# Residual sums of layers 1 and 2: VectorE, or ScalarE and GpSimd

## The chip, the cores and the metric

The kernel runs on one core of a Trainium2 chip. The metric is the device time of one launch in microseconds (us). The kernel before took 6616.1 us, the median of three runs (6615.68 to 6616.88). Differences under 0.2% (13 us) are not told from no change.

The engines are called TensorE (PE in the profile, its weight loads PEld), VectorE (DVE), ScalarE (ACT), GpSimd (POOL) and SyncE (SP). SP here only issues DMAs.

## The reference

Four graph layers over 16 graphs of 1024 nodes with 128 features, each followed by a residual sum and a layer norm. Layers 1 and 2 are the ones concerned.

```python
# layer 1: maximum over the neighbours
def _L1_gnn_ref(x, adj, W, b):
    W1, W2 = (W[:d], W[d:])
    p = einsum('bnd,do->bno', x, W1 - W2)
    q = einsum('bnd,do->bno', x, W2)
    pre = p[:, :, None, :] + q[:, None, :, :] + b
    return max(relu(pre) * adj[..., None], axis=2)

# layer 2: sum over the neighbours, two dense layers
def _L2_gnn_ref(x, adjacency, node_mask, W1, b1, W2, b2, eps):
    x_agg = einsum('bnf,bnm->bmf', x, adjacency)
    h = (1.0 + eps) * x + x_agg
    y = maximum(h @ W1 + b1, 0.0) @ W2 + b2
    return where(node_mask[..., None], y, 0)

x = _layernorm(x + _L0_gnn_ref(...))   # attention over the neighbours
x = _layernorm(x + _L1_gnn_ref(...))
x = _layernorm(x + _L2_gnn_ref(...))
x = _layernorm(x + _L3_gnn_ref(...))   # three SAGE convolutions on a thinned adjacency
```

Layer 3 first thins the adjacency: node by node, in order, each node drops every so-many-th of its remaining neighbours, and a dropped edge vanishes for later nodes too. This thinning depends on the adjacency alone. The kernel calls it the dilation.

## The kernel before, in words

The kernel has a long first stage, in which layers 0, 1 and 2 and the dilation run together, and a second stage for layer 3. The change lies in the first stage.

**The slot loop.** The maximum over neighbours of layer 1 takes most of the work. Its columns are cut into 86 groups (NP) of 12 nodes for each graph, and one group is one slot: 16 x 86 = 1376 slots. In each half of a slot (512 nodes) TensorE selects rows of a table of subset maxima by matrix product (`look_up`, L779, tile pg, two PSUM buffers of two banks), and VectorE folds the result into a running maximum (`best`, L831, 128x1024). TensorE also counts which subset each node needs (L748, tile pm) and ScalarE turns the count into a selection (L749, tile hot, three buffers, made two slots ahead). ScalarE splits the table into a high and a low part (L763, L770).

**Fillers between the slots.** All other work is written as Python generators that are drawn on between the slots. While graph b is in the slot loop, `scores` and `attend` do layer 0 of graph b+1, `tables_of` builds its subset tables on VectorE (L467), and `rest` finishes layers 1 and 2 of graph b-1. A generator asks for an engine before each operation, with an estimated cost; `advance` lets it go on when the slot has room left for that engine (ROOM), when a delay in slots has passed since its last step (0.5 unless `delay` says otherwise, 0 with `same=True`), and, for a product in PSUM, when one of two shared banks is free. So the order of instructions on PE, ACT, DVE and POOL is written out by hand by this planner, from estimates, before the kernel runs; each engine then works through its own list in order. The order on SP is not written out.

**`rest`, the generator that is changed.** It relus the layer 1 maximum (L389), transposes it in two halves of four 128x128 blocks into a shared bank (L395), and adds X on VectorE (L398) into y. `norm` takes statistics on VectorE (L265, eight bn_stats), works out the factors on GpSimd in ten small operations (`norm_factors`, L219 to L228), and normalises on ScalarE (L270, eight activations, asked for 6.5 slots after the factors). For layer 2, X is split into three bf16 parts (L408 on ScalarE, L411 on GpSimd), multiplied by the adjacency (L419, L422), and put through two dense layers (L286, L440). The product py lies in a shared bank in two halves; VectorE multiplies it by the node mask nm (L443) and adds X (L445). `norm` follows again, and the result is stored.

**The dilation on GpSimd.** The nodes are walked in 32 rounds of 32 rows, each round about 43 slots, so two rounds go by in a graph. VectorE prepares a round's counts (L601, L603). GpSimd then walks 31 rows in a chain of small dependent operations (L616 to L626, ten operations for each row):

```python
gp.tensor_scalar(half, mine, half_mask[:, m], rest[:, n:n + 1], op0=ALU.mult, op1=ALU.add)
...
gp.tensor_sub(low[:, n + 1:], low[:, n + 1:], hit[:, n, n + 1:])
```

SP stores the result (L632) and loads it back in another layout (L635, tile hit_p), and VectorE goes on with its transpose (L639), which the planner places about nine slots after the last row. With the next counts (L603) the next round begins.

**The last graph.** When the slot loop ends, `rest` of graph 15 has nothing to run beside: it is drawn on 15 times, then the last of the dilation, then the remainder, and layer 3 begins with the edges of graph 0 (L891, L902, L906).

Of the kernel before, what the change touches and what calls it, by code (L numbers as in the profile page):

```python
# [34 lines left out]
AF = mybir.ActivationFunctionType  # L35
# [4 lines left out]
B, N, D, H2 = 16, 1024, 128, 256  # L40
P = 128
# [30 lines left out]
def tile_graph_layers(ctx: ExitStack, tc, a, out):  # L72
    nc = tc.nc
# [77 lines left out]
    def four(v):  # L151
        return v.unsqueeze(1).to_broadcast([3, 4, P])
# [7 lines left out]
    nm = consts.tile([P, T, B], F32, name="nm")  # L160
# [6 lines left out]
    for b in range(B):  # L167
        q, g = divmod(b, G)
# [19 lines left out]
    X = {}  # L188
# [25 lines left out]
    def norm_factors(st):  # L214

        mv = small.tile([P, 4, T], F32, name="ln_mv")
        mean, apart, var, rs = (mv[:, i, :] for i in range(4))
        gp = nc.gpsimd
        gp.tensor_add(mean, st[:, :, 1], st[:, :, 4])  # L219
        gp.tensor_sub(apart, st[:, :, 1], st[:, :, 4])  # L220
        gp.tensor_scalar(mean, mean, -0.5, 0.0, op0=ALU.mult, op1=ALU.add)
        gp.tensor_mul(apart, apart, apart)
        gp.tensor_add(var, st[:, :, 2], st[:, :, 5])
        gp.tensor_scalar(var, var, 1.0 / D, LN_EPS, op0=ALU.mult, op1=ALU.add)
        gp.tensor_scalar(apart, apart, 0.25, 0.0, op0=ALU.mult, op1=ALU.add)
        gp.tensor_add(var, var, apart)
        gp.tensor_tensor(rs, var, mhalf, op=ALU.pow)
        gp.tensor_mul(mean, mean, rs)  # L228
        return rs, mean
# [6 lines left out]
    def layers_012():  # L236
# [17 lines left out]
        def ask(engine, cost, take=False, give=False, same=False, delay=0.5, after=None, third=False, urgent=False):  # L254
            return engine, cost, take, give or urgent and None, 0 if same else delay, after, third

        def shared(name):
            return psum.tile([P, 512], F32, tag="shared", name=name, bufs=2)


        def norm(dst, src):
            st = small.tile([P, T, 6], F32, name="ln_st")
            for t in range(T):
                yield ask("V", 0.29, same=True)
                nc.vector.bn_stats(out=st[:, t, :], in_=src[:, t, :])  # L265
            yield ask("Pool", 0)
            rs, mean = norm_factors(st)
            for t in range(T):
                yield ask("A", 0.25, same=(t > 0), delay=6.5)
                nc.scalar.activation(dst[:, t, :], src[:, t, :], AF.Identity, bias=mean[:, t:t + 1],  # L270
                                     scale=rs[:, t:t + 1])

        def columns_of(dst, src, first=0.5):
            for h in range(2):
                yield ask("PE", 0.44, take=True, delay=0.5 if h else first)
                p = shared("ptr")
                for t in range(4):
                    nc.tensor.transpose(p[:, t * P:(t + 1) * P], src[:, 4 * h + t, :], ident)
                yield ask("A", 0.59, give=True, same=True)
                nc.scalar.copy(dst[:, halves[h]], p)  # L280

        def product_of(lhsT, rhs, dst, func, bias, delay=0.5):
            for h, s in enumerate(halves):
                yield ask("PE", 0.86, take=True, delay=0.5 if h else delay)
                p = shared("pp")
                nc.tensor.matmul(p, lhsT, rhs[:, s], start=True, stop=True)  # L286
                yield ask("A", 0.6, give=True, same=True)
                if bias is None:
                    nc.scalar.copy(dst[:, s], p)  # L289
                else:  # L290
                    nc.scalar.activation(dst[:, s], p, func, bias=bias)
# [94 lines left out]
        def rest(b):  # L386
            best = ps.pop(b)
            yield ask("A", 1.06, after=("rest", b - 1) if b else None)
            nc.scalar.activation(best, best, AF.Relu)  # L389
            y = w4.tile([P, T, D], F32, name="y1", tag="y")  # L390
            for h in range(2):
                yield ask("PE", 0.44, take=True)
                pt = shared("ph")
                for t in range(4):
                    nc.tensor.transpose(pt[:, t * P:(t + 1) * P],  # L395
                                        best[:, (4 * h + t) * P:(4 * h + t + 1) * P], ident)
                yield ask("V", 0.66, give=True)
                nc.vector.tensor_add(y[:, 4 * h:4 * h + 4, :], X[b][:, 4 * h:4 * h + 4, :],  # L398
                                     pt.rearrange("p (t d) -> p t d", d=D))
            happened["y1", b] = now  # L400
            yield from norm(X[b], y)
            xT = w4.tile([P, N], F32, name="xT2")
            yield from columns_of(xT, X[b])
            left = w4.tile([P, T, D], F32, name="left", tag="y")
            parts = w4.tile([P, 3, T, D], BF, name="parts")
            for k in range(3):
                yield ask("A", 1.05, delay=2.5 if k else 0.5)
                nc.scalar.copy(parts[:, k], left if k else X[b])  # L408
                if k < 2:
                    yield ask("Pool", 0)  # L410
                    nc.gpsimd.tensor_sub(left, left if k else X[b], parts[:, k])  # L411
            hT = w4.tile([P, N], F32, name="hT")
            for h, s in enumerate(halves):
                for c in range(T):
                    yield ask("PE", 0.65, take=(c == 0), same=(c > 0))
                    if c == 0:
                        pa = shared("pa")
                    for k in range(3):
                        nc.tensor.matmul(pa, parts[:, k, c, :], An[b][:, c, s], start=(c == 0 and k == 0),  # L419
                                         stop=(c == T - 1 and k == 2))  # L420
                yield ask("V", 0.66, give=True)
                nc.vector.scalar_tensor_tensor(hT[:, s], xT[:, s], eps1, pa, op0=ALU.mult, op1=ALU.add)  # L422
            del An[b]
            zT = []
            for k, tag in ((0, "xT2"), (1, "parts")):
                z = w4.tile([P, N], F32, name=f"z{k}", tag=tag)
                yield from product_of(W1[:, k * P:(k + 1) * P], hT, z, AF.Relu, b1[:, k:k + 1])
                zT.append(z)
            y = w4.tile([P, T, D], F32, name="y")
            for h in range(2):  # L430
                q = slice(4 * h, 4 * h + 4)
                for half in range(2):
                    yield ask("PE", 1.0, take=(half == 0), same=(half == 1))
                    if half == 0:
                        py = shared("py").rearrange("p (t d) -> p t d", d=D)
                        nc.tensor.matmul(py, ones_b[:3, :], four(b23), start=True, stop=False)
                    for t in range(2 * half, 2 * half + 2):
                        own = slice((4 * h + t) * P, (4 * h + t + 1) * P)
                        for k in range(2):
                            nc.tensor.matmul(py[:, t, :], zT[k][:, own], W2[:, k, :],  # L440
                                             start=False, stop=(t == 3 and k == 1))
                yield ask("V", 0.65, give=True)
                nc.vector.tensor_mul(y[:, q, :], py, nm[:, q, b].unsqueeze(2).to_broadcast([P, 4, D]))  # L443
                yield ask("V", 0.65)
                nc.vector.tensor_add(y[:, q, :], y[:, q, :], X[b][:, q, :])  # L445
            yield from norm(X[b], y)
            nc.sync.dma_start(out=x3[b], in_=X[b])
            happened["rest", b] = now
# [32 lines left out]
        def dilation():  # L481
# [100 lines left out]
            for k in range(K):  # L582
# [18 lines left out]
                nc.vector.tensor_copy(low, p[:B, 0:R])  # L601
                rest = dil.tile([B, R], F32, name="rest")
                nc.vector.scalar_tensor_tensor(rest, p[:B, R:2 * R], 0.5, half_mask[:, own], op0=ALU.add, op1=ALU.mult)  # L603
                given[own_bank] = now + 0.5
                work = [behind]
# [247 lines left out]
        with tc.manual_schedule(engines={mybir.EngineType.PE, mybir.EngineType.Activation, mybir.EngineType.DVE,  # L853
# [3 lines left out]
            finish(B)  # L857
        assert not streams, streams
        last = rest(B - 1)
        for _ in range(15):  # L860
            next(last)
# [21 lines left out]
    def rows_bank(name):  # L883
        return psum.tile([P, 4, D], F32, tag="subset", name=name, bufs=2)
# [246 lines left out]
    for b in range(B):  # L1131
# [3 lines left out]
        for h in range(2):  # L1135
            p = rows_bank("pback")
# [33 lines left out]
```

## Time and profile before

| what | value |
|---|---|
| median of three runs | 6616.1 us |
| profiled execution | 6613.2 us |
| its span | 6611.5 us |
| mean granted TensorE clock | 0.904 |
| stretch of the slot loop | about 137 to 5284 us |
| VectorE, busy share of the span | 80% |
| TensorE, busy share of the span | 86% |
| GpSimd, busy share of the span | 58% |
| ScalarE, busy share of the span | 56% |
| L831, the running maximum | 2720 of 1210 ns |

The shares are means over the whole span; the first stage and layer 3 load the engines quite differently. In the lines shown below, a group of instructions reads: line, engine, operation, what is written and read, shapes, count, then the busy time in us and the mean in ns, then the idle time just before and what ended it. A wait reads: who, waited for whom, us in total, times, longest. A timeline line reads: start in us, length in us, engine, line, operation, tiles, and in brackets the idle time before it. A stretch reads: from and to, its length, then busy us of PE, PEld, DVE, ACT and POOL with counts, the granted clock, the share of the DMA engines, and GB/s.

### The profile page before, as it was taken

How to read it: one execution, taken by the hardware profiler on the slowest of the kernel's cores; microseconds unless marked ns; L12 is line 12 of the kernel's file. 1: busy time of each engine (PE TensorE's matmuls, PEld its weight loads, DVE VectorE, ACT ScalarE, POOL GpSimd, SP SyncE). 2: the span in 40 equal slices, each digit the busy share in tenths (PEclk: the TensorE clock that was granted, in tenths of full speed). 3: DMA queues.
4: the chain of work that ended last, by engine and by line, in shares of the span. 5: the costliest groups of instructions: out<-in, count | busy, mean ns of one | idle time of the engine just before them, and what ended most of it. 6: DMA issues, size and time to landing. Idle time of an engine off the chain costs nothing. (4 is left out here: it accounts for less than half of the span.)

```text
span 6611.5 us, 85916 instructions
## 1 busy us (share of the span) xinstructions
PE 5697.7 (86%) x27306; PEld 2883.8 (44%) x27306; DVE 5317.7 (80%) x8130; ACT 3733.9 (56%) x6537; POOL 3844.7 (58%) x11285
## 2 busy tenths in 40 slices
PE   6989898989898989899888898888888768787986
PEld 3434344444444444444444444444443345555643
DVE  3989899999999999999999999999998834444453
ACT  4656566666666666666666656666655523333841
POOL 2675767676767776766666676767676511110126
PEclk8989898989898989898989899999987779888997
DMA  5121212121212121212112212121110156563635
GB/s 37 14 27 22 30 24 36 20 27 26 28 28 27 27 27 26 28 26 31 28 29 30 27 26 27 26 27 28 25 25 9 32 93 120 105 124 102 230 128 166
DMA packets 478381, 317.02 MB, mean 48 GB/s; under 512 B 301162, under 2 KB 429668, under 8 KB 473828
## 3 DMA queue, kind: packets, MB, share of 16 engines
q0 software_dynamic: 105648, 84.20, 14.6%
q1 hardware_dynamic: 367600, 226.13, 11.7%
q8 instruction: 214, 3.51, 0.2%
q10 hardware_dynamic: 4676, 1.19, 0.1%
q14 instruction: 243, 1.99, 0.1%
HBM read 412.71 MB, written 117.18 MB: 80 GB/s over the span
## 5 line engine op out<-in xcount | busy, mean ns | idle before, releaser
L831 DVE TENSOR_TENSOR best<-best,pg 128x1024 f32<-128x1024 f32 x2720 | 3234.4, 1210 | 309.0 <-PE pg L779 300.5
L749 ACT ACTIVATE hot<-pm,one_less 128x512 fp32r<-128x512 f32 x2752 | 1882.3, 688 | 1115.1 <-PE pm L748 1102.9
L779 PE MATMUL pg<-hot,high 64*128 64x512 f32 x5504 | 1479.1, 534 | 453.6 <-DVE best L831 417.8
L779 PE MATMUL pg<-hot,low 64*128 64x512 f32 x5504 | 1173.3, 423 | 0.0
L748 PE MATMUL pm<-AT,lit 120*128 120x512 fp8e4 x2752 | 1143.8, 416 | 9.3 <-ACT hot L749 6.2
L779 PEld LDWEIGHTS pg<-hot,high 64*128 64x128 f32 x5504 | 547.9, 196 | 1265.1 <-DVE best L831 792.4
L616 POOL TENSOR_SCALAR sc<-low_counts,half_mask,rest 16x1 f32<-16x1 f32 x992 | 435.7, 439 | 399.6 <-DVE rest L603 305.8
L779 PEld LDWEIGHTS pg<-hot,low 64*128 64x128 f32 x5504 | 573.4, 205 | 0.0
L748 PEld LDWEIGHTS <-lit 120*128 120x128 fp8e4 x2752 | 274.5, 100 | 624.8 <-issue 560.8
L621 POOL TENSOR_SCALAR sc<-sc 16x1 f32<-16x1 f32 x992 | 430.1, 434 | 105.0
L770 ACT CAST low<-pt 128x256 fp32r<-128x256 f32 x688 | 255.6, 371 | 396.3 <-PE pt L768 392.1
L980 POOL TENSOR_TENSOR length<-length,mhalf 128x8 f32<-128x8 f32 x48 | 78.9, 1644 | 571.7 <-DVE length L979 571.7
L618 POOL TENSOR_SCALAR sc<-sc 16x1 f32<-16x1 f32 x992 | 341.8, 345 | 107.7
L624 POOL TENSOR_SCALAR last_rank<-V,sc 16x31 f32<-16x31 bf16 (+30 forms) x992 | 387.1, 390 | 0.0
L623 POOL TENSOR_SCALAR hit<-V,sc 16x31 bf16<-16x31 bf16 (+30 forms) x992 | 372.5, 376 | 0.0
L768 PE MATMUL pt<-high,less 128*128 128x256 f32 x688 | 303.2, 441 | 66.3 <-ACT high L763 58.9
L467 DVE TENSOR_TENSOR sub<-sub,q 128x24 f32<-128x24 f32 (+11 forms) x768 | 306.6, 400 | 24.6 <-ACT q L289 10.5
L619 POOL TENSOR_SCALAR sc<-sc 16x1 f32<-16x1 f32 x992 | 270.1, 272 | 83.3
L937 ACT CAST m<-near 128x1024 fp32r<-128x1024 fp8e4 x256 | 253.3, 1044 | 112.7 <-DVE near L906 59.8
L760 PE MATMUL pt<-ident,sub 128*128 128x128 f32 x1376 | 293.9, 298 | 24.7 <-ACT hot L749 22.0
L377 PE MATMUL pav<-v,eT 128*128 128x128 f32 x2048 | 307.6, 296 | 2.1 <-ACT eT L370 2.1
L617 POOL TENSOR_SCALAR sc<-sc 16x1 f32<-16x1 f32 x992 | 256.6, 259 | 86.6
(258 smaller groups left out, 9495.7 us busy)
## 6 DMA issues: line engine op xcount, KB each, us to landing
removed<-gone SPq DMA_DIRECT2D x128, 256.0 KB
An<-in_adj_dram POOLq DMA_DIRECT2D x16, 1024.0 KB, 15.1
E<-in_adj_dram POOLq DMA_DIRECT2D x128, 128.0 KB, 6.8
gone_all<-removed POOLq DMA_DIRECT2D x64, 256.0 KB, 12.1
near<-in_adjT_dram POOLq DMA_DIRECT2D x16, 1024.0 KB, 17.3
h<-x SPq DMA_DIRECT2D x32, 512.0 KB
kept<-near SPq DMA_DIRECT2D x16, 1024.0 KB
share<-share SPq DMA_DIRECT2D x32, 512.0 KB
```

Of the source, the lines that this page charges most:

```text
L377: nc.tensor.matmul(pav, eT[:, c, :], values[b][:, c, :], start=(c == 0), stop=(c == T - 1))
L467: nc.vector.tensor_max(sub[:, :n_g, n:2 * n], sub[:, :n_g, 0:n], qg[:, 2 * g0:2 * g0 + n_g, k:k + 1].to_broadcast([P, n_g, n]))
L616: gp.tensor_scalar(half, mine, half_mask[:, m], rest[:, n:n + 1], op0=ALU.mult, op1=ALU.add)
L618: gp.tensor_scalar(sf, half, 5.5, sf, op0=ALU.is_gt, op1=ALU.mult)
L621: gp.tensor_scalar(to, at, sf, none, op0=ALU.subtract, op1=ALU.subtract)
L623: gp.tensor_scalar(hit[:, n, n + 1:], V[:, n, n + 1:], at, None, op0=ALU.is_equal)
L624: gp.tensor_scalar(last[:, n + 1:], V[:, n, n + 1:], to, None, op0=ALU.is_le)
L748: nc.tensor.matmul(pm, lit[:, r, :], AT[b * (T + 1) + c][:, halves[h]], start=True, stop=True)
L749: nc.scalar.activation(hots[s][:, halves[h]], pm, AF.Relu, bias=one_less)
L768: nc.tensor.matmul(pt, less, high, start=False, stop=True, skip_group_check=True)
L779: nc.tensor.matmul(pg[:, a], part[rows, at * P:(at + 1) * P], hots[s][rows, halves[h]], start=(k == 0), stop=(k == 1))
L831: nc.vector.tensor_max(own, own, pg)
```

## The change

In layer 1, ScalarE copies the transposed maximum from PSUM into y, and GpSimd adds X in place. In layer 2, ScalarE multiplies py by the node mask while it takes it from PSUM, one activation for each of the four 128-column blocks because the mask is a scale for each partition, and GpSimd adds X in place. Before each `norm`, a request for VectorE with a delay of four slots is put in. Nothing else is edited; the planner lays out the other work anew.

```diff
@@ rest, layer 1
-                yield ask("V", 0.66, give=True)
-                nc.vector.tensor_add(y[:, 4 * h:4 * h + 4, :], X[b][:, 4 * h:4 * h + 4, :],
-                                     pt.rearrange("p (t d) -> p t d", d=D))
+                yield ask("A", 0.6, give=True, same=True)
+                q = slice(4 * h, 4 * h + 4)
+                nc.scalar.copy(y[:, q, :], pt.rearrange("p (t d) -> p t d", d=D))
+                yield ask("Pool", 0)
+                nc.gpsimd.tensor_add(y[:, q, :], y[:, q, :], X[b][:, q, :])
             happened["y1", b] = now
+            yield ask("V", 0, delay=4)
             yield from norm(X[b], y)
@@ rest, layer 2
-                yield ask("V", 0.65, give=True)
-                nc.vector.tensor_mul(y[:, q, :], py, nm[:, q, b].unsqueeze(2).to_broadcast([P, 4, D]))
-                yield ask("V", 0.65)
-                nc.vector.tensor_add(y[:, q, :], y[:, q, :], X[b][:, q, :])
+                yield ask("A", 0.9, give=True, same=True)
+                for t in range(4):
+                    nc.scalar.activation(y[:, 4 * h + t, :], py[:, t, :], AF.Copy, scale=nm[:, 4 * h + t, b:b + 1])
+                yield ask("Pool", 0)
+                nc.gpsimd.tensor_add(y[:, q, :], y[:, q, :], X[b][:, q, :])
+            yield ask("V", 0, delay=4)
             yield from norm(X[b], y)
```

## The prediction

> **What bounds the kernel now.** I read the page's busy line first, then the busy time by stretch, since the page mixes two stages.
>
> ```profile
> PE 5697.7 (86%) x27306; PEld 2883.8 (44%) x27306; DVE 5317.7 (80%) x8130; ACT 3733.9 (56%) x6537; POOL 3844.7 (58%) x11285
> ```
>
> ```profile
> 155.00:5140.00 4985.00, 4420.82 (x21568) 2116.79 (x21570) 4568.80 (x6787) 3077.82 (x5653) 3467.31 (x10434) 0.91 0.19 26
> 5284.00:5352.00 68.00, 41.62 (x205) 21.60 (x205) 20.50 (x44) 23.73 (x37) 13.30 (x26) 0.74 0.44 65
> ```
>
> In the slot loop (first row: PE, PEld, DVE, ACT, POOL, clock) VectorE is busy 4568.80 of 4985.00 us, 92%; TensorE 89%, ScalarE 62%, GpSimd 70%. The second row is the last graph's layers 1 and 2, after the loop. The list of waits tells who holds whom:
>
> ```profile
> PEld pg L779 <- DVE best L831: 792.4, 1207, 12.3
> ...
> PE pg L779 <- DVE best L831: 417.8, 423, 12.0
> ...
> POOL sc L616 <- DVE rest L603: 305.8, 32, 36.5
> ...
> DVE best L831 <- PE pg L779: 300.5, 571, 6.7
> ```
>
> ```profile
> DVE hit_T L639 <- DMA hit_p<-hit: 54.2, 9, 11.1
> ```
>
> TensorE waits 1210 us for VectorE's maximum, VectorE only 300 us for TensorE: VectorE sets the pace, with TensorE close behind. The last line is the one place where GpSimd gates VectorE. Every 43 slots GpSimd walks 31 dependent row steps (L616 to L626), the result goes by two DMAs into hit_p, and VectorE stands at L639. One such place, from the timeline (GpSimd's last step, then VectorE):
>
> ```profile
> 3294.80 0.18 POOL L626 TENSOR_TENSOR low_counts<-low_counts,hit 16x1 f32<-16x1 f32 x1
> ```
>
> ```profile
> 3306.35 0.31 DVE L639 STREAM_TRANSPOSE hit_T<-hit_p 128x128 bf16<-128x128 bf16 x1 [5.28 <-DMA hit_p<-hit]
> ```
>
> hit_p is there 3306.35 - 3294.98 = 11.4 us after GpSimd ends; I use 11.2. I read this pair for all 32 rounds (numbered from 0). In even rounds VectorE arrives 17 to 34 us after GpSimd's end, so nothing waits. In odd rounds, the second half of a graph, it arrives after 3.4, 1.6, 11.8, 10.9, 8.3, 4.0, 12.3, 6.0, 13.6, 6.1, 14.7, 9.2, 13.0, 10.1, 14.5 us, and in round 31 before GpSimd's end. Odd rounds are thus tied between GpSimd and VectorE.
>
> **What the Trainium skill says.** "GPSIMD Engine Reference", Key points: GpSimd shares its SBUF interfaces with VectorE and contends with VectorE instructions that have two SBUF inputs. The trace agrees: the 16x1 step L618 has a median of 298 ns beside L831 (one SBUF input), 786 ns beside L445 and 1190 ns beside L561 (two). Here L616, otherwise 0.33 us, stretches under L445:
>
> ```profile
> 2604.75 0.88 POOL L616 TENSOR_SCALAR sc<-low_counts,half_mask,rest 16x1 f32<-16x1 f32 x1
> ...
> 2604.90 0.68 DVE L445 TENSOR_TENSOR y<-y,X 128x512 f32<-128x512 f32 x1
> ```
>
> Same page, Elementwise: a two-input add of 2048 elements takes 4497 ns. The trace has 2127 to 2150 ns for 1024 (L411), which agrees; half is 1.08 us for the 512 of the new add. "ScalarE: Activation LUTs", What ACT_TABLE_LOAD costs: an ACTIVATE takes 186 ns + 0.833 per element, each pointer operand adds 93, back-to-back ones overlap by 93. For 128 elements and two pointers that is 479; L270 shows 491.
>
> **The change, part by part.** The prices are these rows:
>
> ```profile
> L411 POOL TENSOR_TENSOR left<-left,parts 128x1024 f32<-128x1024 f32 x16 | 34.4, 2150 | 164.7 <-ACT parts L408 164.7
> ...
> L280 ACT COPY xT<-ptr 128x512 f32<-128x512 f32 x96 | 56.0, 584 | 87.3 <-PE ptr L278 84.6 <-issue 1.7 <-ACT high L763 0.7
> ...
> L445 DVE TENSOR_TENSOR y<-y,X 128x512 f32<-128x512 f32 x32 | 21.9, 686 | 0.0
> L443 DVE TENSOR_TENSOR y<-py,nm 128x512 f32<-128x512 f32 x32 | 21.9, 683 | 9.2 <-PE py L440 9.1
> L398 DVE TENSOR_TENSOR y<-X,ph 128x512 f32<-128x512 f32 x32 | 21.7, 677 | 9.3 <-PE ph L395 9.1
> ```
>
> 1. *Removed from VectorE.* 32 each of L398, L443, L445; two of each belong to the last graph, after the loop. In the loop: 30 x (0.677 + 0.683 + 0.686) = 61.4 us, on the engine that sets the pace. Not all becomes time, as TensorE is near. Cutting the loop of the trace into pieces of 8 slots and fitting their length, 1 us of VectorE work goes with 0.77 us of length (0.72 to 0.84 for pieces of 2 to 16 slots), and 1 us of waiting at L639 with 1.0 (0.86 to 1.04). So -47 us; bounds 0.5 and 1.0: -31 to -61.
>
> 2. *Added to GpSimd.* 64 adds of 1.08 us = 69 us. Laid side by side, the instruction orders of the two programs put the two L398 replacements of a graph in an even round and the two of L445 in the odd one. Even: 10 us of slack against 2.2; hidden. Odd: GpSimd ends 2.16 us later, less about 0.5 us for each L445 that no longer blocks it, while VectorE arrives about 2 us earlier: it gives back what it gained and waits for the adds on top. The orders show exceptions: in round 3, seven maxima move ahead of L639 and its wait falls from 9.6 to 1.1; in rounds 23 to 29 the ten small norm operations leave the GpSimd round.
>
> 3. *The new wait.* bn_stats (L265) of a sum now waits for a GpSimd add; the planner places it four slots later. Taking before's times for the neighbours in the new order, the add ends 2 to 14 us ahead of bn_stats in even rounds; in odd rounds it is late by 3.0 (round 5), 1.7 (9), 2.3, 2.4, 7.9 (19), 3.1, 2.3, 6.1 (27), 5.2 (29). The maxima queue behind bn_stats, so TensorE stops after two banks. The same lateness counts once: a VectorE already held is less early at L639. Per odd round I take the larger of both waits, with 1 us of relief: 7.8, 1.1, 5.7, 3.3, 4.7, 7.1, 2.8, 8.6, 1.0, 8.4, 0.4, 2.9, 1.3, 5.1, 4.2, 12.4 = 77 us, against 53 before: +24. Without the relief 91, +38. Bounds +10 and +45.
>
> 4. *Added to ScalarE.* 32 copies of 0.584 us and 128 scaled copies: estimated from that ScalarE page, four in a row 386 + 3 x 293 = 1.27 us. In all 19 + 41 = 60 us. I take 0: ScalarE idles 38% of the loop and hot is made two slots, about 7 us, before its use. The activations of norm (L270) can stand up to 6 us behind the later GpSimd, which that lead hides. Bounds -2 (a bank freed earlier) and +10.
>
> 5. *Contention.* About 0.25 two-input VectorE operations start per us, so some 15 of 60 adds meet one and hold it for half an add: +5 us (0 to +10). The trace has it: four L467 beside L411 averaged 1958 ns, where the widest form averages 974.
>
> 6. *After the loop*, on the chain: per layer a copy plus an add replaces one or two VectorE operations: about +1 us each, +2 us (0 to +4).
>
> 7. *Queues.* The hit and hit_p DMAs (L632, L635) change places with neighbours on SP in some 14 rounds. What stands ahead of L632 there is ready at least 48 us before GpSimd's end, so it is not held; I take 0. POOL's loads stand up to 2 us later, and are issued slots ahead: 0.
>
> Sum: -47 + 24 + 0 + 5 + 2 = -16 us. The profiled execution took 6613.2 us (span 6611.5), so 6597; the median of the runs, 6616.1, lies 2.9 above it, so **6600 us**.
>
> **Rivals.**
> - *No relief: GpSimd eats the gain.* The loop is tied in 16 of 32 rounds, and a walk of 129 us moves little by dropping two blockers. -40 (factor 0.65) + 38 + 5 + 2 = +5: 6621. For it: 9 rounds wait already. Against it: L618 beside L445.
> - *TensorE takes over.* Factor 0.5: -31 + 24 + 5 + 2 = 0: 6616. For it: TensorE is 89% busy at a mean clock of 0.91. Against it: 1210 us of waits for VectorE against 300.
> - *Slower: the adds are blocked.* The add reads SBUF twice and is longer than any row step, so it meets L561 (1.2 us) more often. If each of the 28 adds in odd rounds takes 1.1 us more and the relief does not show, the loop gains 31 + 14 us of waiting at L639 and L265: -16 + 45 = +29: 6645. The gain is gone at 0.57 us more per add (1.65 us); slower by 0.2% from 1.05 us more (2.1 us). For it: L618 with L561. Against it: 31 of 32 L411 lie within 2109 to 2143 ns.
> - *The work does not leave VectorE*: excluded, as the new order has none of the 96 there.
>
> **How the numbers follow.** A measurement here tells 0.2% (13 us) from no change. Forecast, faster: 0.42, its own range 6582 to 6603. The first two rivals, within 0.2%: 0.34. The blocked adds, slower: 0.24. Low end: -61 + 20 + 5 + 2 = -34, 6582. High end: near the slower rival, 6642.
>
> **What would show it.** Right: in the loop VectorE loses about 60 us of busy time; the wait at L639 rises from 54 to some 60 to 75; a new wait of L265 for GpSimd of 10 to 30 us; the adds at 1.0 to 1.2 us; the scaled copies at 0.3 to 0.4 us; the stage after the loop 2 us longer. Wrong: adds over 1.6 us, waits at L639 and L265 together over 115 us, or a wait of VectorE for pg (300 us) that grows by 30.

## The result and the profile after

The changed kernel takes 6638.8 us (median of 8 runs, 6631.6 to 6643.5) against 6614.5 us for the kernel before (8 runs beside it): ratio 1.0040, 95% interval 1.0029 to 1.0051. It is **slower by 26 us**. The forecast was 6600 us and faster. Below, a time in us beside a ratio is the ratio's distance from 1, multiplied by the time of the kernel before. When two experiments are compared, their two intervals together make some 0.17%, or 11 us.

The profiled execution took 6631.6 us, the fastest of the eight runs. Its span is 6629.9 us, 18.4 above that before. The mean granted TensorE clock is 0.910, against 0.904 before, so a slower clock is not the cause. In the code of the changed kernel the lines have moved: behind `rest`, each stands five lines further down, so that L561 is now L566, and in the same way L567 is L572, L603 is L608, L639 is L644, L748 is L753, L763 is L768, L779 is L784 and L831 is L836; L440 is L443. First the page's busy line, then the busy time by stretch: the slot loop, and the last graph's layers 1 and 2.

```profile
PE 5664.9 (85%) x27306; PEld 2872.0 (43%) x27306; DVE 5293.3 (80%) x8034; ACT 3772.2 (57%) x6697; POOL 3916.0 (59%) x11349
```

```profile
155.00:5156.50 5001.50, 4393.39 (x21565) 2107.67 (x21563) 4548.54 (x6697) 3113.24 (x5804) 3531.98 (x10493) 0.92 0.19 26
5300.00:5368.00 68.00, 38.81 (x188) 20.08 (x189) 15.15 (x37) 24.98 (x44) 16.91 (x28) 0.72 0.42 56
```

VectorE has 96 instructions fewer, yet only 24 us less busy time (5317.7 before), where some 65 us were taken away. In the loop it loses 20 us and the loop is 16.5 us longer (from the first write of the running maximum to the end of the last one, 5144.1 us before, 5160.6 after). The waits of the changed kernel:

```profile
PEld pg L784 <- DVE best L836: 790.6, 1147, 14.5
PE pg L784 <- DVE best L836: 423.1, 406, 14.2
...
DVE best L836 <- PE pg L784: 333.8, 603, 11.9
...
POOL sc L621 <- DVE rest L608: 252.0, 32, 21.3
...
DVE hit_T L644 <- DMA hit_p<-hit: 42.3, 10, 13.3
...
DVE ln_st L265 <- POOL y L449: 20.3, 8, 8.0
DVE ln_st L265 <- POOL y L401: 12.3, 2, 11.9
```

The wait for the dilation (L639 of before) fell from 54.2 to 42.3; a new one, of bn_stats for GpSimd's adds, is 32.6 us in all: 11 of them lie in the loop, the others after it, in the last graph. VectorE's wait for pg rose from 300.5 to 333.8. The new operations, as groups:

```profile
L449 POOL TENSOR_TENSOR y<-y,X 128x512 f32<-128x512 f32 x32 | 40.5, 1267 | 55.5 <-ACT y L447 55.5
L401 POOL TENSOR_TENSOR y<-y,X 128x512 f32<-128x512 f32 x32 | 40.5, 1267 | 20.2 <-ACT y L399 20.0
L447 ACT ACTIVATE y<-py,nm 128x128 f32<-128x128 f32 x128 | 36.5, 368 | 36.3 <-PE py L443 36.3
L399 ACT COPY y<-ph 128x512 f32<-128x512 f32 x32 | 18.9, 589 | 10.9 <-PE ph L395 10.9
```

The add takes 1267 ns where 1080 were forecast; ScalarE's operations are as forecast. Each of the 64 adds lies between 1250 and 1291 ns: none is held up by VectorE. It is the other way round. One place from the timeline (VectorE's scan, then GpSimd):

```profile
3040.94 2.08 DVE L566 TENSOR_TENSOR_SCAN rank<-E,rank 128x512 f32<-128x512 uint8 x1
...
3040.67 1.27 POOL L401 TENSOR_TENSOR y<-y,X 128x512 f32<-128x512 f32 x1
3041.93 1.23 POOL L621 TENSOR_SCALAR sc<-low_counts,half_mask,rest 16x1 f32<-16x1 f32 x1
```

The scan takes 1243 ns on average in the kernel before. Here it starts 0.27 us into the add and takes 2.08 us, as if most of its work began when the add ended, and the next row step, a 16x1 operation of 0.33 us elsewhere, takes 1.23 us beside it. The Trainium skill, "SBUF — State Buffer", section "SBUF: two separate sides", says that the port pair shared by VectorE and GpSimd is an exclusive lock: of a GpSimd operation and a VectorE operation with two SBUF inputs, whoever starts first has it for the whole instruction and the other blocks. The trace agrees: seven scans beside an add average 2065 ns against 1255 for the other 249, and three L567 average 2149 against 1276. Whenever these ten began, they ended 1.09 to 1.14 us after the add did.

### The profile page after: what moved, and what is told of

The parts are those of the page before. It is cut to its first block, busy times and chain, and to the rows that moved or that the text cites. A ratio compares the mean times of both kernels' runs of the same rounds, so it can differ in the third digit from the quotient of the medians.

```text
span 6629.9 us, 86106 instructions
## 1 busy us (share of the span) xinstructions
PE 5664.9 (85%) x27306; PEld 2872.0 (43%) x27306; DVE 5293.3 (80%) x8034; ACT 3772.2 (57%) x6697; POOL 3916.0 (59%) x11349
## 5 line engine op out<-in xcount | busy, mean ns | idle before, releaser
L836 DVE TENSOR_TENSOR best<-best,pg 128x1024 f32<-128x1024 f32 x2720 | 3232.9, 1211 | 347.1 <-PE pg L784 333.8
L784 PE MATMUL pg<-hot,high 64*128 64x512 f32 x5504 | 1462.8, 528 | 448.3 <-DVE best L836 423.1
L784 PE MATMUL pg<-hot,low 64*128 64x512 f32 x5504 | 1157.9, 417 | 0.0
L753 PE MATMUL pm<-AT,lit 120*128 120x512 fp8e4 x2752 | 1131.4, 411 | 28.5 <-ACT low L775 26.9
L784 PEld LDWEIGHTS pg<-hot,high 64*128 64x128 f32 x5504 | 542.4, 194 | 1278.9 <-DVE best L836 790.6
L784 PEld LDWEIGHTS pg<-hot,low 64*128 64x128 f32 x5504 | 565.4, 202 | 0.0
L753 PEld LDWEIGHTS <-lit 120*128 120x128 fp8e4 x2752 | 274.0, 100 | 610.5 <-issue 547.0
L773 PE MATMUL pt<-high,less 128*128 128x256 f32 x688 | 296.9, 432 | 83.7 <-ACT high L768 75.7
```

The source lines that it names most:

```text
L753: nc.tensor.matmul(pm, lit[:, r, :], AT[b * (T + 1) + c][:, halves[h]], start=True, stop=True)
L784: nc.tensor.matmul(pg[:, a], part[rows, at * P:(at + 1) * P], hots[s][rows, halves[h]], start=(k == 0), stop=(k == 1))
L836: nc.vector.tensor_max(own, own, pg)
```

## The experiments

**First: what the removal and the additions are worth, each by itself.** Four kernels, with edits against before (a0) and after (a1, a2, a3). The fence gives them in short form; `-` marks what is left out:

```diff
a0  -  L398, L443, L445        norm(X[b], y) -> norm(X[b], X[b])
a1  -  copies, scaled copies, adds of the changed kernel; norm reads X
a2  -  nc.gpsimd.tensor_add(y[:, q, :], y[:, q, :], X[b][:, q, :])   (both layers)
a3  -  copies and scaled copies; adds read X twice
```

> The kernel before with its 96 VectorE residual operations (L398, L443, L445) left out and nothing in their place; the norms of layers 1 and 2 read X, so the sums are missing. The planner's requests, and with them the order of all other work, stay as before. What is the removal worth by itself? The forecast's factor of 0.77: -47 us against before (6615), plus 3 for the last graph: near 6566. Theory T (the removed work lies in slots whose length is set by TensorE's own filler, the product py or the transposes ph, so that VectorE only waits for pg instead): no more than half of 61 us, -10 to -30, 6585 to 6605.

Measured: 1.0011 (1.0003 to 1.0019).

> The changed kernel without its copies, scaled copies and GpSimd adds; the norms of layers 1 and 2 read X, so the sums are missing. Same work as the kernel with no residual operation in the order of before, but in the order of the changed kernel, with the four slots of delay. Theory O (the new order is the loss): 15 us or more slower than that kernel. Theory T and theory G (GpSimd's adds are the loss): within 8 us of it.

Measured: 1.0020 (1.0010 to 1.0029).

> The changed kernel without the 64 GpSimd adds: y holds the copies alone, X is not added. Same order. Theory G (the adds hold VectorE at bn_stats, at L639 and through the shared SBUF interface): at least 20 us faster than the changed kernel (6639), below 6619. Theory A (ScalarE's copies, in order ahead of the selections hot, hold TensorE): within 8 us of the changed kernel, and 20 us or more above the kernel with neither.

Measured: 0.9960 (0.9947 to 0.9972), 26 us faster than before.

> The changed kernel without ScalarE's 32 copies and 128 scaled copies; GpSimd adds X to X in their place, so the products are missing from y. Same order, same 64 adds. Theory G: near the changed kernel (6639), within 8 us, and 20 us above the kernel with neither. Theory A: near the kernel with neither.

Measured: 1.0088 (1.0074 to 1.0102).

Three of the four are spoilt: in them the last graph's statistics (L265) stand inside the loop, where in the kernel before they stand after it, and VectorE stood still once in the last graph, for 54.5 us (a0), 66.0 us (a1) and 67.3 us (a3). a2 has no such place; its longest standstill in the loop is 10.4 us. It says that ScalarE's part with all 61 us taken from VectorE is worth 26 us, and that the adds then cost 1.0040 - 0.9960, **52 us**, for 64 adds of 1.27 us.

**Second: the removal without that standstill, and the walk.** b0 and b1 are a0 and a1 with the last graph left as it was. b2 leaves out one of the ten GpSimd operations of each row; b3 is b0 and b2 together.

```diff
b0/b1  as a0/a1, but the operations stay  if b == B - 1
b2  -  gp.tensor_add(hit[:, n, n + 1:], hit[:, n, n + 1:], last[:, n + 1:])
```

> The kernel before with the 90 VectorE residual operations of graphs 0 to 14 left out (61 us of VectorE work; graph 15 keeps its six, so that the end of the loop is as before); the norms of these graphs read X. All orders as before. The earlier run without graph 15's operations had 50 us of standstill in the last graph; graphs 0 to 14 of its trace came out 11 us shorter. Theory R (the odd rounds are gated by GpSimd's walk, so that VectorE work removed in them is waited away at L639) and theory T (TensorE sets the length of those slots): -8 to -25 against before. The forecast's factor: -47.

Measured: 0.9967 (0.9954 to 0.9979), -22 us.

> The changed kernel with the copies, scaled copies and GpSimd adds of graphs 0 to 14 left out, graph 15 kept; the norms of graphs 0 to 14 read X. From the trace of the earlier run, less its standstill: -20 to -35 against before. If so, the kernel with the products alone (-26) shows ScalarE's part as 0 to +10, and the GpSimd adds as about +50, most of the change's loss. Theory O (the new order costs): slower than the same removal in the order of before by 8 us or more.

Measured: 0.9958 (0.9945 to 0.9972), -28 us.

> The kernel before with GpSimd's step L625 left out of every row (the two sets of hits are not joined, so other edges are dropped; no later time depends on that). A round's walk is some 31 x 0.28 = 9 us shorter, so GpSimd gates nearly no round: the wait at L639 falls from 54 us to under 20. -20 to -40 against before. It is the reference for the next kernel.

Measured: 0.9889 (0.9874 to 0.9904), -73 us, where 20 to 40 were expected.

> The kernel with the shorter walk, and also without the 90 VectorE residual operations of graphs 0 to 14. Theory R: with GpSimd out of the way the removal is worth the forecast's 0.77, -35 to -50 against the kernel with the shorter walk alone. Theory T: the removal is worth no more than it is with the full walk, within 8 us of that difference (-8 to -25), and VectorE's wait for pg grows by 25 us or more.

Measured: 0.9826 (0.9813 to 0.9840), -115 us.

In b0, 61 us less on VectorE give 22 us (0.36 of it), in b1 28 us (0.46). The new order of the work is thus not what costs: with the sums gone, it is no slower than the old one. The waits of b0:

```profile
DVE best L831 <- PE pg L779: 308.7, 555, 9.1
...
DVE hit_T L639 <- DMA hit_p<-hit: 82.9, 14, 15.2
```

The wait at L639 rose from 54.2 to 82.9, that for pg by 8 only: VectorE came earlier, and GpSimd did not. In b1, in the new order, it is the other way round: by its trace VectorE stands idle 29 us at the transpose, and 28 us more than in the kernel before ahead of the maxima. With the shorter walk of b2 the wait at L639 is gone from the list, and the same removal (b3 against b2) is worth 0.9889 - 0.9826, 42 us (0.68). a2 against b1 (0.9960 and 0.9958) says that ScalarE's copies and products cost 1 us in this order of the work, give or take 12.

**Third: one layer at a time.** c0 has layer 1 of the changed kernel and layer 2 of before; c1 has layer 1 of before and layer 2 of the changed kernel. c2 is the changed kernel with X of layer 2 added by VectorE. c3 is the changed kernel with the short walk of b2.

```diff
c2 (layer 2)  -  yield ask("Pool", 0); nc.gpsimd.tensor_add(...);  yield ask("V", 0, delay=4)
              +  yield ask("V", 0.65); nc.vector.tensor_add(y[:, q, :], y[:, q, :], X[b][:, q, :])
```

> Layer 1 as in the changed kernel (ScalarE copies, GpSimd adds X, four slots of delay ahead of the norm), layer 2 as in the kernel before. The GpSimd adds then lie in even rounds alone, where VectorE comes to L639 17 to 34 us after GpSimd's end. Theory R (an add costs time where GpSimd's walk gates VectorE): 20 us leave VectorE at some 0.45 us of time each, and the 32 adds cost a few us of shared access: -5 to -12 us, ratio 0.998 to 0.999. Theory E (every add costs the same, wherever it stands, some 0.8 us of time, because GpSimd and VectorE share access to SBUF): 32 adds cost 25 us: +15 us, ratio 1.002.

Measured: 1.0011 (1.0002 to 1.0019).

> Layer 2 as in the changed kernel (four scaled copies by ScalarE, GpSimd adds X, delay of four slots), layer 1 as in the kernel before. All 30 adds of the loop lie in odd rounds. Theory R: nearly all of the loss of the changed kernel is here: +20 to +35 us, ratio 1.003 to 1.005, with the waits at L639 and at L265 as in the changed kernel (together some 60 to 75 us). Theory E: half of the cost of the adds, two thirds of the removal: +5 to +10 us, ratio about 1.001.

Measured: 1.0031 (1.0019 to 1.0042). The two parts add up to the whole: 7 + 20 us against 26. The waits of c1:

```profile
DVE best L833 <- PE pg L781: 322.8, 550, 8.3
...
DVE ln_st L265 <- POOL y L446: 57.0, 17, 8.0
...
DVE hit_T L641 <- DMA hit_p<-hit: 48.4, 11, 11.2
```

Both waits together are 105 us, where 60 to 75 were expected: in the odd, tied rounds bn_stats now waits for layer 2's adds, 48 us in the loop and 9 in the last graph. But theory R fails on layer 1: adds in even rounds, where VectorE comes 17 to 34 us late anyway, should have been nearly free and c0 5 to 12 us faster. It came out 7 us slower, which is under 0.2% and not called a loss here, but it is no gain. All held scans (ten, mean 1806 ns) are found in c0; in c1 not one lies beside an add.

> Layer 1 as in the changed kernel; in layer 2 ScalarE takes the products, and VectorE adds X as it did before (no GpSimd add there, no delay). The whole result is computed. 41 us leave VectorE in the loop instead of 61. Theory R: no add in a tied round, so about 0.45 x 41 = -18 us, ratio 0.996 to 0.998: faster than both kernels. Theory E: -18 + 25 = +7 us, ratio 1.001. If what hurts is ScalarE's part in layer 2 (the bank of py is freed later or earlier, and TensorE's products move against VectorE), it is near the changed kernel, 1.003.

Measured: 1.0008 (0.9999 to 1.0016). Theory R fails here again. In the loop VectorE also waited 29 us at its add of X for ScalarE's product, since the planner puts the add right behind it.

> The changed kernel with the ninth of the ten GpSimd operations of each row (hit plus last) left out, so the second drop of each row is not carried out. To be read against the kernel before with the same short walk (6549 us, ratio 0.9889). With GpSimd out of the way, theory R: the removal is worth -40 us, the adds keep only their shared access (+12) and ScalarE's part (up to +14): -15 to -25 us against that, ratio 0.985 to 0.987; waits at L639 and at L265 for GpSimd near 0. Theory E: the adds still cost 50 us: +10 us against it, ratio 0.990 to 0.991.

Measured: 0.9889 (0.9876 to 0.9903), the same as b2. With the walk out of the way the loss is gone, but no gain has come; this lies between the two theories.

**Fourth: the two waits taken away.** d0 leaves layer 1 as it was, has the products on ScalarE, and adds X on VectorE two slots later. d1 is the changed kernel with one number changed.

```diff
d0 (layer 2)  -  yield ask("V", 0.65); nc.vector.tensor_add(...)
              +  yield ask("V", 0.65, delay=2); nc.vector.tensor_add(...)
d1 (layer 2)  -  yield ask("V", 0, delay=4)
              +  yield ask("V", 0, delay=7)
```

> Layer 1 as in the kernel before; in layer 2 ScalarE takes the products, and VectorE adds X two slots later (in the mixed kernel it stood directly behind and VectorE waited 29 us for ScalarE there). GpSimd gets nothing new; the whole result is computed. 20 us leave VectorE in the loop. If the GpSimd adds are what makes the changed kernel slow: 20 x 0.4 = -8 us, up to -15 with fewer blocked GpSimd steps: ratio 0.9977 to 0.999, faster than both kernels. If the products on ScalarE are what costs (they stand in ScalarE's queue ahead of the table's high and low parts, and TensorE waits for these): +5 to +15 us, ratio 1.001 to 1.002.

Measured: 1.0001 (0.9992 to 1.0009). This is neither of the two: 20 us are off VectorE and nothing is new on GpSimd, and yet there is no gain.

> The changed kernel with seven slots of delay in place of four ahead of the second norm, so that bn_stats comes after GpSimd's add has ended. If the wait at L265 (20 us for the layer 2 adds) is time of its own: -15 to -20 us against the changed kernel, ratio about 1.001 to 1.002. If VectorE then waits at L639 or for pg instead, because the round is tied anyway: within 5 us of the changed kernel, ratio about 1.004, with the wait at L639 up by most of what L265 loses.

Measured: 0.9986 (0.9979 to 0.9994), 9 us faster than before and 36 us faster than with four slots. The waits of d1:

```profile
DVE best L836 <- PE pg L784: 325.8, 581, 12.8
...
DVE hit_T L644 <- DMA hit_p<-hit: 22.4, 5, 9.0
DVE ln_st L265 <- POOL y L401: 12.8, 2, 12.5
DVE ln_st L265 <- POOL y L449: 9.4, 2, 8.0
```

I had expected the wait at L265 to go, or to turn up at L639. It went (what is left lies in the last graph), and L639 fell by 20 us as well. The trace points to a reason: `norm_factors` of layer 2, ten small GpSimd operations, follows bn_stats, and with seven slots it left the walk of four more odd rounds. Reading for each round what stands between GpSimd's first and last row step: before, all odd rounds from 3 to 29 hold two sets of norm operations; after, ten of these 14; d1, six. In seven kernels (a2, after, c0, c1, d1, and e0 and e1 below) 47 of these rounds hold one set, and in none of the 47 does VectorE wait at L639. In these seven and before, 65 hold two sets, and in 45 of the 65 it waits.

**Fifth: is it the sums at all?** e0 adds one line to the kernel before, e1 has ten slots in the changed kernel, e2 is d0 with ten slots. f0 is e1 without the adds.

```diff
e0 (before, layer 2)  +  yield ask("V", 0, delay=11)
                         yield from norm(X[b], y)
```

> The kernel before with one line added: eleven slots of delay ahead of the second norm. No sum is moved. In the order of instructions the ten small norm operations of layer 2 then stand behind GpSimd's walk in every odd round from round 3 on (in the kernel before they stood inside it in all 14, in the changed kernel in 10, with seven slots of delay in 6). Theory W (what an odd round costs is set by what stands inside GpSimd's walk): the wait at L639 falls from 54 to some 20 us (rounds 1 and 31 stay), -25 to -35 us, ratio 0.995 to 0.996. Theory S (the gain with the longer delay came from the moved sums, and needed only the wait at L265 gone): no change, ratio 0.999 to 1.001.

Measured: 0.9930 (0.9917 to 0.9942), **46 us faster** than before, with no sum moved, and more than theory W expected. In the two traces the loop is 39 us shorter: VectorE idles 32 us less at L639 and 7 us less ahead of the maxima. From GpSimd's first row step to its last, an odd round (3 to 29) takes 126.4 us on average, where it took 129.7.

> The changed kernel with ten slots of delay in place of four ahead of the second norm: no norm operation of layer 2 is left inside the walk of an odd round. Theory W: a little faster than with seven slots (0.9986), as the wait at L639 falls from 22 to some 17 us: ratio 0.997 to 0.9985; and slower than the kernel before with its own longer delay by what the adds cost in shared access and in the walk less what the removal brings: +5 to +20 us against it. Theory S: as with seven slots, 0.9986, and faster than the kernel before with a longer delay.

Measured: 0.9972 (0.9962 to 0.9983), as theory W has it; but against e0 it is 28 us slower, where 5 to 20 were expected.

> ScalarE takes the products of layer 2, VectorE adds X two slots later, layer 1 as before, and ten slots of delay ahead of the second norm: both levers with nothing new on GpSimd; the whole result is computed. Theory W: the best of these kernels, a further 0 to 10 us below the kernel before with the delay: ratio 0.9935 to 0.996. If the products give nothing even with the walk out of the way (as they did without the delay, 1.0001): equal to the kernel before with the delay.

Measured: 0.9934 (0.9921 to 0.9948), equal to e0. e0 and e2 are the fastest here that leave nothing out, ahead of both the kernel before and the changed one.

> The changed kernel with ten slots of delay and without the 64 GpSimd adds, so X is not added in layers 1 and 2: ScalarE's part alone, with no norm operation of layer 2 inside the walk of an odd round. To be read against the changed kernel with ten slots (0.9972) and the kernel before with its delay (0.9930). If an add costs only by a wait in a tied round, there is none left to pay, and the two differ by the held scans and the end alone, 10 to 15 us: ratio 0.995 to 0.9957, no faster than the kernel before with the delay. If the adds cost the same as without the delay (52 us between 0.9960 and 1.0040): ratio 0.989 to 0.990.

Measured: 0.9947 (0.9933 to 0.9961).

The waits of e0, then those of e1:

```profile
DVE best L832 <- PE pg L780: 295.0, 532, 9.1
...
DVE hit_T L640 <- DMA hit_p<-hit: 22.0, 2, 13.4
```

```profile
DVE best L836 <- PE pg L784: 330.9, 589, 12.6
DVE hit_T L644 <- DMA hit_p<-hit: 19.8, 2, 10.1
```

In both, only rounds 1 and 31 still wait at L639. So the gain of the longer delay belongs to the place of the second norm and not to the sums. The delay moves the whole norm, bn_stats on VectorE and the activations on ScalarE too; that it is the ten GpSimd operations that count is read from the rounds, and no run moved them alone. Between e0 and e1 the change costs 1.0042 (0.9972 / 0.9930), 28 us, as much as between before and after; there is no L639 or L265 wait left in the loop to blame. f0 splits the 28 us: 11 for ScalarE's part with all of the sums taken from VectorE (0.9930 to 0.9947), 17 for the adds (0.9947 to 0.9972). Each is good to some 11 us, so the first is not told from 0; what is clear is that taking the sums from VectorE brings no gain here. Of the adds' 52 us between a2 and the changed kernel about 35 thus go away when the second norm is moved, and 17 stay.

**Where the freed time goes.** From the trace of the loop of e0 and e1, VectorE's time not covered by the instruction before: the removed operations took 55 us, and 9 us went into L561 and L567 held by adds. The wait before the maximum rose by 42 us, and the maxima themselves cover 14 us more, as they overlap less with their predecessors. Waiting for pg takes the place of most of the removed work. It shows as idle spells of 1 to 2 us just before a maximum:

| kernel | such spells in the loop | us |
|---|---|---|
| before / e0 | 20 / 20 | 28 / 27 |
| c0, layer 1 changed | 27 | 37 |
| b1, no sums up to the last graph | 40 | 54 |
| c1, layer 2 changed | 52 | 68 |
| a2 / f0, ScalarE's part | 48 / 51 | 60 / 64 |
| after / e1 | 54 / 54 | 67 / 67 |

In the changed kernel 26 of the 54 lie at slots 60 to 64 of a graph, where TensorE makes most of py; in the kernel before none lies there. In c1, where py is made at slots 58 to 62, only four lie at slots 60 to 64 and most of the others at 65 to 73, which these experiments do not explain. One of the 26, from the timeline (ScalarE, TensorE, VectorE):

```profile
2621.76 1.14 ACT L447 ACTIVATE y<-py,nm 128x128 f32<-128x128 f32 x4 [1.06 <-PE py L443]
2622.78 0.70 ACT L754 ACTIVATE hot<-pm,one_less 128x512 fp32r<-128x512 f32 x1
2623.34 0.40 ACT L768 CAST high<-pt 128x256 fp32r<-128x256 f32 x1
...
2623.79 0.38 PE L773 MATMUL pt<-high,less 128*128 128x256 f32 x1 [0.97 <-ACT high L768]
...
2625.11 5.92 DVE L836 TENSOR_TENSOR best<-best,pg 128x1024 f32<-128x1024 f32 x5 [1.02 <-PE pg L784]
```

ScalarE stands 1.06 us for py with four products at the head of its list; hot and the high part of the table, which TensorE needs next, come after. TensorE then waits 0.97 us, and VectorE 1.02. In the kernel before, VectorE has its own L443 and L445 at slots 60 to 62. b1 has the same order but no products in these graphs: of its 40 spells 10 lie at slots 60 to 64, against 24 in a2, which has the products. So the products add spells at this place, though a2 is not slower than b1 by the runs. How the 11 us of f0 divide between the products, the new order and TensorE's own pace was not measured.

## Why the prediction was wrong

The forecast was -47 us for the removal, +31 for the adds (24 of waits, 5 of contention, 2 at the end) and 0 for ScalarE. The runs give -28 (b1), +52 (from a2 to the changed kernel) and +1 (from b1 to a2), together about the measured 26. So two terms failed, the removal by 19 us and the adds by 21, each give or take some 11. Either one put right alone would have made the forecast "no change"; only both make it slower.

- **Step 1, the removal, failed.** -47 us was 61.4 times 0.77, a factor fitted over all of the loop. The removed work stands at two special places, though, and there it was worth 22 to 28 us (0.36 to 0.46), outside even my bound of -31. In the old order VectorE waited the time away at GpSimd's walk (b0: L639 up by 29 us; the factor is 0.68 with the shorter walk of b3), in the new order for pg. A slope over many slots says what an average microsecond is worth, not one in these slots.
- **Steps 2 and 3, the adds and the new wait, failed too.** The add is 1.27 us, not half of L411's 2.13, for a forecast of 1.08. I forecast 77 us for both waits in the loop, 24 above before; the trace has 42 and 11 there, 53 as before. That is no relief: a2 has 33 and 0, so the adds bring back 21 us of waiting there, and 52 us by the runs. The traces of a2 and of the changed kernel, whose profiled execution was its fastest, are only 33 us apart; the 21 us of waiting, 10 of held VectorE operations and 5 after the loop account for these, and the rest of the 52 is in no trace. That the waits are below the forecast fits a VectorE that comes later to these places because the removal was worth less; this was not tested. What I did not ask is why odd rounds are tied. I noted that ten norm operations would leave the walk in rounds 23 to 29, and they did; moving the second norm in all odd rounds from 3 on is worth 46 us with no sum moved, and I took it as a by-product.
- **Step 4, ScalarE at 0.** It is 1 us by a2 and b1, give or take 12, so the step held as far as this tells. With the odd rounds relieved, its part together with the removal gives no gain (f0, +11 us, not told from 0), where step 1 would have the removal alone gain. I looked at the lead of hot and not at high, for which TensorE's own wait (L773 after, L768 before) rose from 58.9 to 75.7 us; but it is 68.9 in b1 too, so the products make a part of that at most.
- **Step 5, contention.** The forecast was 5 us. By the trace, seven L561 (0.81 us each), three L567 (0.87) and one each of L540 and L467 (0.86 and 1.09) make 10 us, my upper bound. I thought that half an add would be waited for; in the trace the scan may wait for a GpSimd DMA issue, the add, and then hold the next row step (one scan reached 3.14 us).
- **Step 6, the end.** The forecast was 2 us, and 2.7 were measured (1330.1 to 1332.8 from the end of the last maximum on).
- **Step 7, the queues.** No experiment tried it, but the traces agree with 0: in the rounds 0 to 30 that wait at L639, VectorE goes on 11.5 us after GpSimd's end before and 11.4 after.
- **The rivals.** "The adds are blocked" had the right sign and size (+29) by luck: its mechanism is not there, as no add is over 1.29 us. "No relief" is what b0 shows, where GpSimd's walk eats half of the removed time, and "TensorE takes over" (factor 0.5) is what b1 and the changed kernel show; but their sums, +5 and 0, lack what the adds cost. Of the signs set out, the one for a wrong forecast that came true is the wait for pg, up by 33 where 30 was the mark.

## What to carry to other kernels

Before you price work that is taken off the busiest engine, go to the very places where it stands and ask what that engine meets next: here, in the old order, half of it was waited away at another engine's walk, and in the new order much of it at a matmul. Where two engines hand a round back and forth, list everything that stands inside the round on the slower one and move out what need not be there: one line of delay gave 46 us, while moving 96 operations lost 26. An operation moved to GpSimd costs its own time there, and here it also held the scans and other VectorE operations with two SBUF inputs that started beside it.

## What was not expected of the hardware

A VectorE scan with two SBUF inputs that starts beside a GpSimd add does not share with it but runs after it: 2.08 us for 1.24, up to 3.14 us where a GpSimd DMA issue of 1.03 us stood ahead of the add; the small GpSimd operation behind it is then held in turn, 1.23 us for 0.33. VectorE's maximum, with one input in PSUM, takes 1214 ns on average beside such an add and 1211 elsewhere. A GpSimd add of 512 elements takes 1.27 us, more than half of a subtraction of 1024 (2.13).
